# Three early blocks of gathers instead of two in a two-batch attention and deformable-convolution kernel, with more background calls while the early image is built

## The chip, the cores and the metric

The kernel runs on one core of one Trainium2 chip. The metric is the device time of one execution in microseconds (us). All data are float32.

## The reference, cut to what matters

The input x is two images of 256 channels, 64 x 64 pixels. Four layers follow one another:

- Layer 0: group norm, self-attention with 4 heads of 64 channels over the 4096 pixels, a projection, and the residual.
- Layer 1: a position term, added.
- Layer 2, the bottleneck: a 1x1 convolution to 64 channels, a 3x3 *deformable* convolution with a mask, a 1x1 convolution back to 256 channels, the residual and a ReLU.
- Layer 3: twice a group norm with ReLU and a 3x3 deformable convolution of 256 channels, whose offsets come from a 7x7 depthwise convolution and a 1x1 convolution; then the residual.

A deformable convolution reads its input at places that are known only at run time:

```python
off = off.reshape(B, KK, 2, H, W)
py = yy + ky + off[:, :, 0]; px = xx + kx + off[:, :, 1]
sampled = bilinear_gather(x, py, px)        # four corners, weighted
out = einsum('bckhw,ock->bohw', sampled, w)
```

## The kernel before, in words

`Net.run` calls `attention`, then `deform`. On TensorE (PE), VectorE (DVE), ScalarE (ACT) and GpSimd (POOL) the instructions stand in the order in which the Python code issues them. On SyncE (SP), which issues most of the plain DMAs, the order is left to a scheduler.

**Attention.** There are four units of work: (batch 0, heads 0 and 1), (batch 0, heads 2 and 3), and the same for batch 1. A unit has 256 steps n, 1024 in all, and the main loop takes two steps at a time, a *pair*. A step is a block of scores (L580, PE), its row minimum (L592, DVE), the exponentials (L598, ACT), their transposition (L610, PE) and copies (L627 DVE, L629 ACT), and the product with the values (L639, PE). POOL combines the parts of a block (L519 to L525).

What doesn't belong to a step is put between the steps in two ways. The dictionary `own` holds functions with the step at which they are due: loads, keys and values of the next unit, the projection, the first 1x1 convolution of layer 2. And `back` holds generators, the background, in order: `background(count)` (L661) goes through the list and takes up to `count` yields; a generator that yields False passes the turn to the next one. In a pair there are up to three such calls: one for each of the two steps without an own function (from unit 2 on), and one at the end of the pair.

In unit 2 `first_batch` joins the background: the deformable convolution of layer 2 for batch 0 (`conv`, with its gathers on POOL), and then `early_image` (L1180). That normalizes the result for batch 0 (L1192, ACT), stores it (L1197), transposes it (L1204, PE), copies it (L1209, DVE) into buffers `bfour`, and stores those as the image `img3` (L1214), from which layer 3 gathers: 25 yields, eight blocks i of one part for the activations and two for the transposes. In unit 3 `before` of batch 1 is put at the head of the list, and `early_samples` (L1218) at its end. That computes for the first `EARLY` blocks of layer 3 (a block is 512 pixels) the offsets (`offsets`, 28 matrix products per block at L805, then L825, L839 and the small DVE operations of `corners`), and queues 36 gathers per block: 9 taps by 4 groups of 128 pixels, each gather 128 rows of 4 KB. From then on `self.sample`, called once or twice at the end of a pair (11 times in 16 steps), issues one gather on POOL (L848) into one of the buffers in `free`, and on SP the store (L1261) of an earlier one to the scratch `samp_d` in HBM. There are three buffers (`xb`) until the offsets of the last early block are done, nine from then on. The main loop runs until n has passed 1028, the background is empty, nothing is due and no sample is left.

**Deform.** Layer 3, as 1152 samples s: two batches times two layers, each of 8 blocks of 36 samples. For a sample the kernel brings 128 x 1024 floats (`four`), weighs the four corners (ACT and DVE), transposes (L1508, PE), copies (L1517, ACT) and multiplies (L1527, PE). The 72 samples of the early blocks are loaded from `samp_d` (L1448, SP; the first 8 by POOL's queue); the others are gathered by POOL (L848, `four<-img,didx`). An early sample is weighed corner by corner: ACT scales the first (L1486), DVE adds the other three (L1496, three instructions). The other samples of the first layer of batch 0 are `paired`: ACT scales two corners at once (L1471), DVE adds the other two (L1477), and then one more of each (L1486, L1490). `gather` runs 8 samples ahead (`AHEAD`) into ten buffers.

Beside the first samples runs `conv` for batch 1: the second run of layer 2's deformable convolution, 144 steps, each with two gathers on POOL (`bfour<-img,bidx`, L848), a weighing (L1067) and two additions (L1077, L1078) on DVE, and after every fourth step a transposition (L1088) and its copy. It gathers seven steps ahead, into eight buffers. Its pace is set by a `Side`: at sample s it has had `rate * s + more(s)` yields; it has two yields per step, after 7 leading yields. When it is done, the second image is built from its result.

Of the kernel before, what the change touches and what calls it, by code (L numbers as in the profile page):

```python
# [25 lines left out]
K2 = 9  # L26
EPS = 1e-5
DWK = 7

EARLY = 2  # L30


GH, GW = H + 1, W + 2
# [31 lines left out]
class Net:  # L65
    def __init__(self, ctx, tc, a, out):
        self.tc, self.nc, self.a, self.out = tc, tc.nc, a, out
        nc = self.nc
        const = ctx.enter_context(tc.tile_pool(name="const", bufs=1))
        self.small = ctx.enter_context(tc.tile_pool(name="small", bufs=2))  # L70
        dram = ctx.enter_context(tc.tile_pool(name="dram", bufs=1, space=DRAM))

        self.ident = const.tile([P, P], F32, name="ident")
        make_identity(nc, self.ident)
        self.vec = const.tile([P, V_COLS], F32, name="vec")
        nc.sync.dma_start(self.vec, a["vec"])
        self.sel = const.tile([P, 32], F32, name="sel")
        self.shift = const.tile([P, DWK, 32], F32, name="shift")
        self.later = [(self.sel, a["sel"]), (self.shift, a["shift"])]

        self.img2, self.img3, self.x2d = [], [], []

        self.xn_d, self.xa_d = [], []
        for b in range(B):
            self.img2.append(dram.tile([GH * GW, 2 * CM], F32, name=f"img2_{b}"))
            self.img3.append(dram.tile([GH * GW, 2 * C], F32, name=f"img3_{b}"))
            self.x2d.append(dram.tile([C, HW], F32, name=f"x2d_{b}"))
            self.xn_d.append(dram.tile([C, HW], F32, name=f"xn_{b}"))
            self.xa_d.append(dram.tile([C, HW], F32, name=f"xa_{b}"))

        self.pos_d = dram.tile([C, HW], F32, name="pos_d")

        self.samp_d = [dram.tile([4 * K2 * P, 4 * C], F32, name=f"samp_d{i}") for i in range(EARLY)]
        self.sample = lambda: False
        self.early = {}
        self.share_d = [dram.tile([16, P], F32, name=f"share_d{n}") for n in range(2)]

        vec = self.vec
        self.bn_s = const.tile([P, 4], F32, name="bn_s")
        self.bn_t = const.tile([P, 4], F32, name="bn_t")  # L100
        rstd = self.rsqrt(vec[:, V_BNV : V_BNV + 4], 4)
        nc.vector.tensor_mul(self.bn_s, rstd, vec[:, V_BNG : V_BNG + 4])
        m = self.small.tile([P, 4], F32, name="bn_m")
        nc.vector.tensor_copy(m, vec[:, V_BNM : V_BNM + 4])

        nc.vector.tensor_sub(m[:, 1:2], m[:, 1:2], vec[:, V_DCNB : V_DCNB + 1])
        nc.vector.tensor_mul(m, m, self.bn_s)
        nc.vector.tensor_sub(self.bn_t, vec[:, V_BNB : V_BNB + 4], m)

        for v in (self.bn_s, self.bn_t):  # L110
            nc.vector.tensor_copy(v[CM:P, 0:2], v[0:CM, 0:2])
# [69 lines left out]
    def attention(self, bott):  # L181
# [5 lines left out]
        with ExitStack() as ctx:  # L187
# [489 lines left out]
            while n < last + 4 or back or more or any(own.values()):  # L677
                u, d = divmod(n, per_unit)
                if d == 0 and u < len(units):
                    plan_unit(u)  # L680
                    if u == 0:
                        back.append(prepare(1))
                    if u == 1:
                        back.append(bott.before(0, bt, ps))
                    if u == 2:
                        back.append(first_batch())
                    if u == 3:
                        back.insert(0, bott.before(1, bt, ps))
                        back.append(self.early_samples(bott, bt, held, xp, vp, kp, ps))

                def small(at):
                    steps = own.pop(at, ())
                    for f in steps:
                        f()
                    if not steps and u > 1:
                        background(1)

                if n - 1 in pts:
                    p = pts.pop(n - 1)
                    keep(n - 1, p, "ACT")  # L700
                    keep(n - 1, p, "DVE")
                ps.flush()
                sc = [scores(m) for m in (n + 2, n + 3) if m < last]
                for m in range(len(sc)):
                    lowest(n + 2 + m, sc[m])
                if n < last:
                    p = turn(e.pop(n))
                    keep(n, p, "DVE")
                if sc:
                    e[n + 2] = exponentials(n + 2, sc[0])  # L710
                if n < last:
                    keep(n, p, "ACT")

                small(n)
                if 4 <= n < last + 4:
                    attend(n - 4)
                    attend(n - 3)
                small(n + 1)
                if n < last:
                    pts[n + 1] = turn(e.pop(n + 1))  # L720
                if sc:
                    e[n + 3] = exponentials(n + 3, sc[1])
                if u or n % 8 == 0:
                    background(1)

                for _ in range(1 + (n % 16 in (10, 12, 14))):
                    more = self.sample()
                n += 2


    def corners(self, i, pt, mask, base, idx, w4, pool, w=None):

        nc = self.nc
        p = pool.tile([P, 4, K2, 2], F32, name="pos")
        off = pt[:, :, 0 : 2 * K2].rearrange("p j (k t) -> p j k t", t=2)
        nc.vector.tensor_tensor(p, off, base[:, 4 * i : 4 * i + 4], ALU.add)
        if mask:
            mk = pool.tile([P, 4, K2], F32, name="mask")  # L740
            nc.vector.tensor_scalar_max(mk, pt[:, :, 2 * K2 : 3 * K2], -87.0)
        yield False
        if mask:

            nc.scalar.activation(mk, mk, AF.Exp, scale=-1.0)

        nc.vector.tensor_scalar(p, p, float(H), -1.0, ALU.min, ALU.max)
        whole = pool.tile([P, 4, K2, 2], I32, name="whole")
        nc.vector.tensor_copy(whole, p)
        yield True  # L750
        f = pool.tile([P, 4, K2, 2], F32, name="floor")
        nc.vector.tensor_copy(f, whole)
        g = pool.tile([P, 4, K2, 2], F32, name="above")
        nc.vector.tensor_tensor(g, f, p, ALU.is_gt)
        yield False
        nc.vector.tensor_tensor(f, f, g, ALU.subtract)
        nc.vector.tensor_scalar_min(f, f, float(H - 1))
        if w is None:
            w = pool.tile([P, 2, 4, K2, 2], F32, name="wt")
        nc.vector.tensor_tensor(w[:, 1], p, f, ALU.subtract)  # L760
        yield False
        nc.vector.tensor_scalar(w[:, 0], w[:, 1], -1.0, 1.0, ALU.mult, ALU.add)
        at = g.rearrange("p j k t -> p (j k t)")[:, : 4 * K2]
        at = at.rearrange("p (j k) -> p j k", k=K2)
        nc.vector.scalar_tensor_tensor(
            at, f[:, :, :, 0], float(GW), f[:, :, :, 1], ALU.mult, ALU.add
        )
        nc.vector.tensor_scalar_add(idx, at, float(GW + 1))
        yield True
        if mask:  # L770
            nc.vector.tensor_scalar_add(mk, mk, 1.0)
            nc.vector.reciprocal(mk, mk)
            yield False
            for s in range(2):
                nc.vector.tensor_mul(w[:, s, :, :, 1], w[:, s, :, :, 1], mk)
            yield False
        for s in range(4):
            nc.vector.tensor_mul(w4[:, :, :, s], w[:, s % 2, :, :, 0], w[:, s // 2, :, :, 1])
        yield True
# [76 lines left out]
    class Bottleneck:  # L856
# [41 lines left out]
            self.od = wp.tile([P, 512], F32, name="bod")  # L898
            nc.gpsimd.memset(self.od, 0.0)

        def pools(self, ctx, gathers=5, sums=8):
            self.ahead = gathers - 1
            tc = self.net.tc
            return self.kept | {
# [275 lines left out]
    def early_image(self, bott, pools, ps):  # L1180

        nc, x2d = self.nc, self.x2d[0]
        sc, sh = self.norm_scale(bott.stats[0], bott.gmask, V_GN_G[0], V_GN_B[0], ps)
        yield True
        v = self.img3[0].rearrange("(y x) (s c) -> y x s c", x=GW, c=C)
# [31 lines left out]
    def early_samples(self, bott, pools, held, xp, vp, kp, ps):  # L1217
# [38 lines left out]
        def gather():  # L1256


            if len(stores) > 1 and len(free) < 3 or not gathers and stores:
                dst, four = stores.popleft()  # L1260
                nc.sync.dma_start(dst, four)  # L1261
                free.append(four)
# [8 lines left out]
        for i in range(EARLY):  # L1271
# [22 lines left out]
                load(i + 1)  # L1294
            if i + 1 == EARLY:
                free.extend(whole)
            for m in range(4 * K2):
                k, j = divmod(m, 4)
                gathers.append((self.samp_d[i][m * P : m * P + P, :], idx[:, j, k : k + 1]))

    def deform(self, bott):
# [5 lines left out]
        with ExitStack() as ctx:  # L1307
# [287 lines left out]


            last = Side(0, 1, bott.last(1, bott.kept, ps))
            seconds = Side(0, 0.9, second, lambda s: 2.5 * min(s, EARLY * BLOCK))
            stats[0] = self.norm_stats()
            images = []  # L1600
            for s in range(ALL + 12):
# [135 lines left out]
```

## Time and profile before

| what | us |
|---|---|
| median of 3 runs (5137.35 to 5144.84) | 5140.26 |
| the profiled execution | 5136.46 |
| its span, first to last instruction | 5134.7 |
| last exponential of attention (L598) starts | 2960.2 |
| first sample gather, last sample gather in attention | 2612.8, 2908.9 |
| first sample weighed in deform (L1486) | 2989.5 |
| first gather of the second `conv` on POOL | 2997.5 |

| engine | busy, us | share of the span |
|---|---|---|
| PE | 4802.3 | 94% |
| DVE | 4012.2 | 78% |
| ACT | 3255.6 | 63% |
| POOL | 2336.0 | 45% |

The profile is one execution. Its page gives the busy time of the engines, the span in 40 slices with the busy share of each in tenths, and groups of instructions: line, engine, operation, output and inputs, count, then busy time and mean ns of one, then the engine's idle time before them and what ended it. PEld is the weight load of PE; DMA is the mean share of the 16 DMA engines. "issue" is time in which an engine waited for nothing that the profile shows. Other views cut the same trace by window, by line, or list it in order of time; all their times count from the start of the span.

### The profile page before, as it was taken

The page shows a single profiled execution, that of the slowest core. Times are in us where ns is not written, and L with a number is a line of the kernel's source. Part 1 is how long each engine was busy: PE and PEld are TensorE (multiplying, and loading weights), DVE is VectorE, ACT ScalarE, POOL GpSimd, SP SyncE. Part 2 cuts the span into 40 slices and gives each one's busy share as a digit, 9 for nine tenths or more (in the row PEclk, how much of TensorE's full clock was granted, in tenths as well). Part 3 has the DMA queues.
Part 4 walks back from the last instruction along what each step waited for, and adds up shares of the span by engine and source line. Part 5 has one row for each costly group of instructions (what it writes and reads, how often), then busy time and mean ns, then how long its engine had stood idle before and what let it go on. Part 6 is the DMA issues. An engine that isn't in the chain of part 4 may idle for free. (4 is left out here: it accounts for less than half of the span.)

```text
span 5134.7 us, 100400 instructions
## 1 busy us (share of the span) xinstructions
PE 4802.3 (94%) x38200; PEld 2665.6 (52%) x38200; DVE 4012.2 (78%) x7281; ACT 3255.6 (63%) x5869; POOL 2336.0 (45%) x2256
## 2 busy tenths in 40 slices
PE   8999999999999999999999956679999999999998
PEld 5555565555565555565555523234444444454444
DVE  6878767878768888677766768867788888888888
ACT  5676656666667666666656622257876766666666
POOL 0111111111106777564023257775776666666665
PEclk9999999999999999999999978889999999999999
DMA  5231121111112333322557667679999999999998
GB/s 172 61 97 52 43 69 49 35 47 30 55 53 85 100 100 103 96 84 74 158 172 277 251 237 238 204 243 359 349 327 341 358 368 349 359 401 345 350 353 329
DMA packets 367026, 997.69 MB, mean 194 GB/s; under 512 B 61372, under 2 KB 98810, under 8 KB 366542
## 3 DMA queue, kind: packets, MB, share of 16 engines
q0 software_dynamic: 196560, 690.41, 37.7%
q1 hardware_dynamic: 169438, 300.73, 18.0%
q8 instruction: 300, 4.92, 0.4%
q14 instruction: 184, 1.51, 0.1%
q10 hardware_dynamic: 544, 0.13, 0.0%
HBM read 855.36 MB, written 127.35 MB: 191 GB/s over the span
## 5 line engine op out<-in xcount | busy, mean ns | idle before, releaser
L598 ACT ACTIVATE e<-sc,low 128x1024 f32<-128x1024 f32 x1024 | 1147.3, 1120 | 739.1 <-DVE low L592 736.2
L848 POOL DMA_INDIRECT four<-img,didx x1080 | 1163.2, 1077 | 558.1 <-issue 132.8
L592 DVE TENSOR_REDUCE low<-sc 128x1 f32<-128x1024 f32 x1024 | 1204.5, 1217 | 229.9 <-PE sc L580 225.3
L1527 PE MATMUL out<-st,wc 128*128 128x512 f32 x2304 | 1234.0, 618 | 118.2 <-ACT st L1517 100.7
L580 PE MATMUL sc<-k,qs 64*128 64x512 f32 x2048 | 998.0, 605 | 1.8 <-ACT e L598 1.4
L639 PE MATMUL av<-et,v 128*64 128x256 f32 x8192 | 996.6, 385 | 0.0
L580 PE MATMUL sc<-k,q 64*128 64x512 f32 x2048 | 977.0, 604 | 0.0
L519 POOL TENSOR_TENSOR o<-o,f 128x1024 f32<-128x1024 f32 x63 | 149.6, 2375 | 1763.4 <-DMA f<-share_d 966.5
L610 PEld LDWEIGHTS tt<-ident,e 64*128 64x128 f32 x16384 | 654.5, 139 | 512.4 <-issue 271.6
L629 ACT COPY et<-tt 128x512 f32<-128x512 f32 x1152 | 659.5, 585 | 171.4 <-PE tt L610 170.3
L1496 DVE SCALAR_TENSOR_TENSOR smp<-four,dw,smp 128x256 f32<-128x256 f32 x1296 | 627.2, 484 | 176.0 <-ACT smp L1486 144.9
L610 PE MATMUL tt<-ident,e 64*128 64x64 f32 x16384 | 726.5, 226 | 35.5 <-ACT et L629 18.3
L627 DVE COPY et<-tt 128x512 f32<-128x512 f32 x896 | 611.6, 683 | 161.7 <-PE tt L610 161.3
L639 PEld LDWEIGHTS av<-et,v 128*64 128x64 f32 x8192 | 553.2, 137 | 300.7 <-issue 47.8
L1508 PEld LDWEIGHTS pt<-ident,smp 128*128 128x128 f32 x2304 | 330.1, 144 | 661.6 <-issue 458.5
L848 POOL DMA_INDIRECT bfour<-img,bidx x576 | 583.5, 1013 | 183.5 <-issue 90.6
L1527 PEld LDWEIGHTS out<-st,wc 128*128 128x128 f32 x2304 | 389.9, 195 | 388.6 <-issue 201.2
L1471 ACT ACTIVATE four<-four,dwt 128x512 f32<-128x512 f32 x648 | 463.5, 715 | 192.6 <-DMA four<-img,didx 188.8
L1477 DVE SCALAR_TENSOR_TENSOR four<-four,dwt 128x512 f32<-128x512 f32 x648 | 483.8, 747 | 105.5 <-ACT four L1471 103.2
L1508 PE MATMUL pt<-ident,smp 128*128 128x128 f32 x2304 | 448.9, 277 | 27.2 <-DVE smp L1496 26.0
L580 PEld LDWEIGHTS sc<-k,qs 64*128 64x128 f32 x2048 | 346.2, 188 | 209.1 <-issue 116.3
L805 PE MATMUL pd<-x,wf 128*126 128x512 f32 x840 | 435.1, 600 | 0.0
(189 smaller groups left out, 4738.1 us busy)
## 6 DMA issues: line engine op xcount, KB each, us to landing
f<-share_d SPq DMA_DIRECT2D x128, 256.0 KB
four<-samp_d SPq DMA_DIRECT2D x64, 512.0 KB
xb<-xn SPq DMA_DIRECT2D x55, 512.0 KB
img<-imgt SPq DMA_DIRECT2D x96, 256.0 KB
four<-img,didx POOLq DMA_INDIRECT x1080
xa<-res SPq DMA_DIRECT2D x32, 512.0 KB
samp_d<-xb SPq DMA_DIRECT2D x32, 512.0 KB
xb<-in_x SPq DMA_DIRECT2D x20, 512.0 KB
```

Source lines behind the costliest of these rows:

```text
L580: nc.tensor.matmul(s[:, j, :], lhsT=q[u, i // 2][int(h != j)][halves[j], at : at + P], rhs=k[u][c][halves[j], h, :], start=True, stop=True,)
L592: nc.vector.tensor_reduce(low, s, AX.X, ALU.max, negate=True)
L598: nc.scalar.activation(e.rearrange("p j n -> p (j n)"), s, AF.Exp, bias=blk.low[:, g, c : c + 1], accum_out=blk.sum[:, g, c : c + 1],)
L610: nc.tensor.transpose(pt[:, m, :], e[half, m // 4, m % 4 * P : m % 4 * P + P], self.ident[half, half],)
L627: nc.vector.tensor_copy(dst, pt)
L629: nc.scalar.copy(dst, pt)
L639: nc.tensor.matmul(now["av"][halves[h], :], lhsT=v[u][c][:, m, halves[h]], rhs=ets[j][:, m, h, :], start=(m == 0), stop=(m == 7),)
L848: self.nc.gpsimd.indirect_dma_start(out=dst, out_offset=None, in_=img, in_offset=bass.IndirectOffsetOnAxis(ap=idx, axis=0),)
L1477: nc.vector.scalar_tensor_tensor(uv, four[:, 2 * C :], share(s, 1, 1), uv, ALU.mult, ALU.add)
L1496: nc.vector.scalar_tensor_tensor(smps[s], four[:, c], weight(s, c), smps[s], ALU.mult, ALU.add)
L1508: nc.tensor.transpose(pts[u][:, c, j * P : (j + 1) * P], smp[:, c * P : c * P + P], self.ident,)
L1527: nc.tensor.matmul(outs[ob], lhsT=wc[k][:, c, ob * P : ob * P + P], rhs=sts[u][:, c, :], start=(k == 0 and c == 0), stop=(k == K2 - 1 and ...
```

## The change

Five things change.

- `EARLY` is 3 instead of 2. A third block of offsets and 36 more gathers and stores are issued in attention; `deform` loads 108 early samples instead of 72, computes one block of offsets less, and weighs block 2 corner by corner instead of paired. The pool of corner buffers (`CORNERS`) grows from 11 to 12.
- `self.hurry` is 2 from the start of `early_image` until the offsets of the first early block are done, and 0 otherwise. The call at the end of a pair takes `1 + hurry` yields.
- `gather` of the early samples stores the oldest sample as soon as two are out, not only when fewer than three buffers are free.
- The second `conv` is paced over 108 samples: `1.6 * min(s, 108)` in place of `2.5 * min(s, 72)`, beside the unchanged rate of 0.9.
- `corners` keeps `whole` and `above` in one buffer, and attention's `conv` has 7 buffers `bsmp` instead of 8.

```diff
-EARLY = 2
+EARLY = 3
...
+        self.hurry = 0
...
-                    background(1)
+                    background(1 + self.hurry)
...
-        whole = pool.tile([P, 4, K2, 2], I32, name="whole")
+        whole = pool.tile([P, 4, K2, 2], F32, name="whole").bitcast(I32)
...
-        g = pool.tile([P, 4, K2, 2], F32, name="above")
+        g = whole.bitcast(F32)
...
-        def pools(self, ctx, gathers=5, sums=8):
+        def pools(self, ctx, gathers=5, sums=7):
...
     def early_image(self, bott, pools, ps):
         nc, x2d = self.nc, self.x2d[0]
+        self.hurry = 2
...
-            if len(stores) > 1 and len(free) < 3 or not gathers and stores:
+            if len(stores) > 1 or not gathers and stores:
...
                 free.extend(whole)
+            self.hurry = 0
             for m in range(4 * K2):
...
-            seconds = Side(0, 0.9, second, lambda s: 2.5 * min(s, EARLY * BLOCK))
+            seconds = Side(0, 0.9, second, lambda s: 1.6 * min(s, EARLY * BLOCK))
```

## The prediction, made before the changed kernel was built or run

> **What bounds the kernel now.** I read first the 40 slices of the page (128.4 us each).
>
> ```profile
> PE   8999999999999999999999956679999999999998
> DVE  6878767878768888677766768867788888888888
> POOL 0111111111106777564023257775776666666665
> DMA  5231121111112333322557667679999999999998
> ```
>
> PE is full in attention (slices 1 to 22) and DMA is full from slice 27 on. Between them, slices 23 to 26, neither is: that is where the first blocks of `deform` run beside the second `conv`, and it is the only stretch with room. The start times of `first` (L1486) give its blocks of 36 samples: block 0 begins at 2989.5, block 1 at 3152.6, block 2 at 3319.1, block 3 at 3437.1, block 4 at 3523.3; after that a block takes 57 to 61. So blocks 0 to 3 take 163, 167, 118 and 86 us, 534 together. The view of these windows:
>
> ```profile
> core 0: us, PE busy (x) PEld busy (x) DVE busy (x) ACT busy (x) POOL busy (x), PEclk, DMA share, GB/s
> 2989.00:3152.00 163.00, 89.68 (x271) 41.77 (x270) 132.03 (x315) 35.48 (x67) 117.34 (x114) 0.74 0.76 250
> 3152.00:3319.00 167.00, 116.36 (x361) 52.67 (x360) 146.93 (x334) 42.99 (x78) 129.06 (x125) 0.79 0.68 216
> 3319.00:3437.00 118.00, 77.33 (x240) 36.73 (x239) 77.94 (x166) 53.80 (x93) 91.47 (x87) 0.84 0.71 227
> 3437.00:3523.00 86.00, 69.17 (x237) 33.42 (x236) 61.51 (x141) 55.24 (x96) 51.80 (x48) 0.89 0.88 307
> ```
>
> POOL issues 125 gathers in 167 us and 87 in 118: 1.34 and 1.36 us each. A group of its own row shows why that is its limit although it is "busy" only 77%:
>
> ```profile
> L848 POOL DMA_INDIRECT bfour<-img,bidx x230 | 238.9, 1039 | 77.5 <-issue 37.2 <-DVE smp L1496 8.5 <-DMA x<-xn 8.3
> ```
>
> A gather takes 1.04 us and the timeline has 0.30 us behind each, whatever is named as releaser. So blocks 0 to 2 are bound by POOL's issue; DVE follows closely (147 of 167 us). Block 3 is mixed, with DMA at 0.88. What DVE does there (groups of 2989 to 3437):
>
> ```profile
> L1496 DVE SCALAR_TENSOR_TENSOR smp<-four,bw,smp 128x256 f32<-128x256 f32 x216 | 104.3, 483 | 9.9 <-DMA wc<-in_dcw 4.2 <-ACT smp L1486 0.5
> L1067 DVE TENSOR_TENSOR bfour<-bfour,bw 128x512 f32<-128x512 f32 x135 | 92.4, 685 | 34.6 <-DMA bfour<-img,bidx 34.5
> L1077 DVE TENSOR_TENSOR bfour<-bfour 128x256 f32<-128x256 f32 x135 | 57.0, 422 | 2.9
> L1078 DVE TENSOR_TENSOR bsmp<-bfour 128x128 f32<-128x128 f32 x135 | 39.5, 293 | 10.1
> ```
>
> The 0.2% that separates faster and slower from no change is 10 us here.
>
> **Deform: the gain.** `conv` has 144 steps of two gathers and two yields, after 7 leading yields. Its allowance at sample s is 0.9 s + 2.5 min(s, 72) before, 0.9 s + 1.6 min(s, 108) after. At s = 108 that is 277 yields before (135 steps, as the x135 above), 270 after (131 steps, with 7 more gathered ahead: 138 steps, 277 gathers). Before, POOL had also to issue 36 image gathers for block 2 and 8 for block 3; after, block 2 comes by SP from `samp_d`, so 8 remain. POOL: 285 x 1.34 = 382 us, and its first gather starts 8 us after block 0 (2997.5): 390. DVE: it was busy 132 + 147 + 78 = 357. Block 2 is no longer paired: 36 x (0.750 + 0.481) = 44 go, 36 x 3 x 0.483 = 52 come; four conv steps of 1.40 go (6). That is 359 us, and it can't be hidden by POOL any more: with the first wait for a gather (15.4 on the chain of waits), the 4.2 for `wc` and some 15 of small gaps it needs 393. Two engines at 390 and 393 that feed each other through 8 buffers: I take 400, 48 less than 448. Ends: 390 if they overlap perfectly, and 359/0.88 + 15 = 423 if DVE gets no fuller than in block 1, so -58 to -25. Block 3 has 12 conv steps instead of 9 and 47 gathers instead of 48; its DVE work rises by 5 us, which mostly lies beside the gathers: +3. Starting the second image some 8 samples later costs nothing: its 53 steps at 0.9 a sample end near s = 204, before 228 where they are forced. From block 4 on DMA is full and nothing changes. **Deform -45** (-58 to -20). The loads added on SP, 36 of 512 KB, replace gathers of the same size; DMA at 0.7 hides them. If that cover went, 36 x 1.58 us (57/36, the pace of full DMA) = 57 us would be at stake; that it is bound by POOL at 0.7 speaks against it.
>
> **Attention: what is paid.** PE is full there, so work added on PE is paid in full. Windows of attention (image; two blocks' offsets; sampling):
>
> ```profile
> 2449.00:2555.00 106.00, 100.25 (x1002) 60.46 (x1004) 72.88 (x118) 73.50 (x134) 9.22 (x7) 0.98 0.59 171
> 2578.00:2698.00 120.00, 116.93 (x1040) 65.67 (x1038) 70.45 (x133) 63.53 (x119) 28.52 (x27) 0.99 0.56 192
> 2698.00:2877.00 179.00, 174.62 (x1882) 105.08 (x1880) 126.55 (x205) 121.54 (x229) 58.67 (x56) 0.98 0.77 283
> ```
>
> (1) Block 2's offsets. By the exponentials of L598, 32 steps n of attention take 120 us with two blocks' offsets (second row), and 64 take 179 with sampling alone (third), 89.5 for 32. So a block costs (120 - 89.5)/2 = 15 us. PE's own row agrees:
>
> ```profile
> L805 PE MATMUL pm<-v,bx 128*126 128x512 f32 (+3 forms) x56 | 23.3, 573 | 0.0
> ```
>
> is 11.7 a block, and the seven shifted sums and the transposes add some 2.5. **+15** (13 to 17). The same work leaves `deform`, where PE was at 55 to 70%: no gain.
>
> (2) The squeezed image. Written out by the code's rules, the loop gives for before: image n = 852 to 886, first sample at 902, last at 1004; the trace has the first sample gather at 2612.8 and the last at 2908.9, between the exponentials of those n. With `hurry` a pair has up to five calls instead of three: image 852 to 866, blocks ready at 872, 882 and 888, samples 872 to 1026, and the loop ends at 1040 in both. The work is the same (64 transposes, 11.6 us of PE), but in 14 n it must pass SP, which the timeline shows full at such a pace:
>
> ```profile
> 2492.20 0.55 SPq L911 DMA_DIRECT2D bx<-x2d  x1
> 2492.79 0.50 SPq L1197 DMA_DIRECT2D xn<-bx  x1
> 2493.38 6.17 SPq L1214 DMA_DIRECT2D img<-bfour  x8
> 2499.65 0.55 SPq L911 DMA_DIRECT2D bx<-x2d  x1
> ```
>
> That is 7.45 us an image block, 60 for eight. Attention meanwhile takes 14 x 2.8 + 11.6 = 51. So the five `bfour` buffers fill and DVE's copies (L1209) wait some 9 us, with the steps n queued behind them on DVE; three calls in a row share one bank, where PE waited 0.58 + 0.37 us for the activation (timeline at 2491), 7 times 0.95 at worst, half of it beside the other wait. **+12.** Low end 0 (no gain: nothing is removed). High end: nothing overlaps, each block waits for 1.52 us of activation and two copies of 0.69, 8 x 2.9 = 23, plus SP's 9: 32, plus 6 us of landing (the upper end on the chain of waits) for each of two loads of `xs` that PE's matmuls follow directly: 44.
>
> The Trainium skill, "DMA: Bandwidth & Descriptors", section Specifications, puts the limit of HBM for one core at about 358 GB/s. An estimate by it: the image moves 16.8 MB (8 loads and 8 stores of 512 KB, 64 of 128 KB), which beside attention's own 50 GB/s (500 to 1000 us) would need 55 us, so about +4 where I have SP's +9, and the sum would be -19 by it. The trace has a slice at 401 GB/s, above that limit, so I let SP decide.
>
> (3) Sampling over 154 n instead of 102. The stretch 2698 to 2784 with samples takes 86 us for 32 n, the last, 2877 to 2961, with few, 84 for 31.5: 0. Storing as soon as two samples are out moves waiting from POOL (57 us before the gathers) to SP (160 us behind L1261 in 2700 to 2960); both have `f`, `q` and `xb` behind them, needed 11 n (30 us) or more later. 0, up to +5.
>
> (4) The end. The last sample is issued 22 n later, near attention's end, and its buffers become `deform`'s. Between 2961 and 2989 DMA is at 0.67; three or four samples of 1 MB at 283 GB/s are 13 us, mostly in the free third. **+4** (0 to 13). The bitcast, the seventh `bsmp` and the larger corner pool remove no instruction and lengthen no wait that I find: 0.
>
> **Sum.** -45 + 15 + 12 + 4 = -14. The profiled execution took 5136.5 (span 5134.7 and 1.8 around it), 3.8 under the median of 5140.3. I carry the difference to the median: 5126.
>
> **Rivals.**
> A, it is slower: the hurried image stalls attention. Place: PE waiting for L1192's activations, L1209's copies and the `xs` loads between n = 852 and 888. Price 44 in place of 12: -45 + 15 + 44 + 4 = +18, 5158. It decides from 26 us on, where the sum is zero. For it: DVE, ACT and PE are in order and SP is full already in the dense part. Against: PE was idle 13 us only from 2440 to 2700, with up to three steps a pair.
> B, DVE takes POOL's place: its work in blocks 0 to 2 isn't reduced at all (357 and 359). At 88% busy the gain is 22 and the sum +9: 5149. For it: 34.5 us of its idle time waits for landings. Against: those come from POOL being late.
> C, the squeeze is free and the two engines overlap well: -52 + 15 + 2 + 1 = -34: 5106. For it: SP's order isn't the program's, and `load(0)` was issued at 2478, 100 us ahead of its use.
> D, the early samples aren't done by attention's end and the loop goes on (the count says 1026 of 1040): a pair's 5.6 us each; 6 pairs would be +34 on the forecast, 5160.
>
> **Chances.** Forecast 0.42 (own range -28 to -2: 5112 to 5138), C 0.20, B 0.17, A 0.18, D 0.03. Faster by over 10 us: 0.72 of the forecast and all of C, 0.50. Within 10: the rest of the forecast and most of B, 0.27. Slower: A, D and the worse part of B, 0.23. The range leaves out the far ends of A and C: 5094 to 5162.
>
> **What would show it.** Right: first sample gather near exponential 874 and the last near 1026; attention's end 22 to 32 us later; 36 fewer `four<-img,didx` (1044), 100 loads from `samp_d` on SP; blocks 0 to 2 near 133 each, block 3 near 89; DVE above 88% there; 57 a block after. Wrong: blocks 0 to 2 over 141 (B), attention over 45 us later with PE idle at L1204 or L805 (A), bare gathers after the last exponential (D).

## The result, and the profile after

The changed kernel takes 5154.95 us (median of 10 runs, 5150.14 to 5164.9), the kernel before 5139.4 (10 runs): a ratio of 1.003, 95% interval 1.002 to 1.004. The forecast was 14 us faster; it is 15.5 us slower. The profiled execution took 5164.9, ten above its median.

The slices of the page, as in the prediction:

```profile
PE   8999999999999999999899966768999999999998
POOL 0111111111107777474023347775766666666666
DMA  5231121111113333322667787879989999999998
```

The full part of PE has a dent now, in slice 19 (2452 to 2581 us, counted from 0 as in the prediction): that is where the image and the offsets stand. The stretch between attention and full DMA is still there, slices 23 to 26. From the start times of the exponentials (step n of attention) and of `first` (the samples of deform), both lists by line:

| stretch | before | changed | difference |
|---|---|---|---|
| n = 848 to 912: image, offsets | 233.2 | 266.8 | +33.6 |
| n = 912 to the last exponential's start | 308.3 | 321.4 | +13.1 |
| from there to deform's first sample | 29.3 | 49.9 | +20.6 |
| deform, blocks 0 to 2 | 447.6 | 380.1 | -67.5 |
| deform, blocks 3 and 4 | 147.6 | 166.9 | +19.3 |

Up to block 4's end that is 18 us more (the two executions reach n = 848 at 2418.7 and 2417.7, so the seventh `bsmp` and the shared buffer of `corners` cost nothing up to there). The rest took 10 more in this execution. In the profiles of the experiments on chips of the same kind it takes 1552 to 1564 us with the changed deform and 1550 to 1554 with the old one, so part of that ten is scatter; a few us of it may be real, and no run looks into them.

The view by windows for blocks 0 to 4 of the changed kernel:

```profile
core 0: us, PE busy (x) PEld busy (x) DVE busy (x) ACT busy (x) POOL busy (x), PEclk, DMA share, GB/s
3055.90:3181.60 125.70, 81.85 (x235) 36.30 (x234) 109.07 (x270) 34.06 (x65) 90.41 (x85) 0.66 0.81 275
3181.60:3301.50 119.90, 84.27 (x262) 37.92 (x261) 113.33 (x249) 34.20 (x64) 92.79 (x90) 0.83 0.81 263
3301.50:3435.90 134.40, 96.81 (x321) 43.74 (x320) 126.50 (x292) 38.87 (x73) 103.76 (x98) 0.86 0.77 248
3435.90:3532.60 96.70, 72.47 (x237) 34.47 (x236) 68.27 (x146) 53.75 (x94) 63.27 (x62) 0.86 0.74 248
3532.60:3602.80 70.20, 62.47 (x236) 31.84 (x235) 52.93 (x118) 56.95 (x98) 38.83 (x37) 0.95 1.01 381
```

DVE is busy 349 of 380 us in blocks 0 to 2, 92%, and POOL issues a gather per 1.39 us: the two balance, as forecast. But POOL got through only 273 gathers there and left 62 to block 3 (it had 48 before); block 3 takes 10 us more. Block 4 takes 9 more: the second image starts 16 us into it (before: 6 us ahead of it), and one of its activations waits 5.9 us for its load. That these two make the +19 is read from the profile; no run separates them.

### The profile page after: what moved, and what is told of

Same layout as the page of the kernel before. It is cut to its first block, busy times and chain, and to the rows that moved or that the text cites. A ratio compares the mean times of both kernels' runs of the same rounds, so it can differ in the third digit from the quotient of the medians.

```text
span 5163.1 us, 100511 instructions
## 1 busy us (share of the span) xinstructions
PE 4819.4 (93%) x38200; PEld 2665.8 (52%) x38200; DVE 4020.7 (78%) x7317; ACT 3231.7 (63%) x5833; POOL 2334.1 (45%) x2256
## 5 line engine op out<-in xcount | busy, mean ns | idle before, releaser
L849 POOL DMA_INDIRECT four<-img,didx x1044 | 1122.2, 1075 | 560.3 <-issue 136.3
L849 POOL DMA_INDIRECT bfour<-img,bidx x576 | 589.5, 1023 | 185.1 <-issue 92.3
L1474 ACT ACTIVATE four<-four,dwt 128x512 f32<-128x512 f32 x612 | 437.7, 715 | 152.0 <-DMA four<-img,didx 149.5
L1480 DVE SCALAR_TENSOR_TENSOR four<-four,dwt 128x512 f32<-128x512 f32 x612 | 456.9, 746 | 84.1 <-ACT four L1474 82.1
L806 PE MATMUL pd<-x,wf 128*126 128x512 f32 (+3 forms) x812 | 417.8, 597 | 0.0
```

What stands on the lines that cost most here:

```text
L806: nc.tensor.matmul(pd[:m, r0 * W : r1 * W], lhsT=wt(s, t), rhs=src[:, (y + r0 - y0) * W : (y + r1 - y0) * W], start=(n == 0), stop=(n == l ...
L849: self.nc.gpsimd.indirect_dma_start(out=dst, out_offset=None, in_=img, in_offset=bass.IndirectOffsetOnAxis(ap=idx, axis=0),)
```

## The experiments

Theory T after the first look: deform gains what was forecast, and attention loses it in four places: the third block of offsets on PE, the squeezed image, late f tiles while samples run (`f` holds the factors with which POOL combines a block's parts; SP loads it from `share_d`), and the end. Each ratio is to the kernel before, timed on the same chip. The groups came from five chips; on three of them the kernel before takes 5141 to 5143 us, on two 5316 and 5320, so kernels are compared within a group.

### First group (before: 5142.74)

**e1_lazy**, the old store rule.

```diff
-            if len(stores) > 1 or not gathers and stores:
+            if len(stores) > 1 and len(free) < 3 or not gathers and stores:
```

> The changed kernel with the store rule of before (a sample is stored only when fewer than three buffers are free); all else as changed. Theory T, from the trace of the changed kernel against the one before: the loss has four places: third block of offsets on PE in attention (+15), the squeezed image (+18), late f tiles while sampling (+12), and the last f tile, which SP issues behind sample stores (+21); deform gains 48 as forecast. Under T the store rule moves only part of the last two: 0 to 10 us less than the changed kernel, the wait of the last combine (22.7 us in the changed kernel) still 10 to 23. Rival R1, the store rule alone makes both the sampling and the end late: 25 us less or more, and the first sample of deform 30 us after the last exponential instead of 49.

5156.37 us, 1.0029 (1.0018 to 1.0039): as the changed kernel. n = 912 to the last exponential 318.8 instead of 321.4, the end 48.2 instead of 49.9. The store rule is not the cause, save for 2 to 3 us; R1 falls.

**e2_hurry2**, before with hurry alone.

```diff
-                    background(1)
+                    background(1 + self.hurry)
...
+        self.hurry = 2
...
+            self.hurry = 0
```

> The kernel before with hurry alone (two early blocks, old stores, old pace). T: steps n = 848 to 912 take 250 us instead of 233 (stalls of PE behind activations, copies and image stores), all samples out by n = 974, nothing else changes: 5152 to 5160 where before is 5139, deform as before. Rival R2, the calls in a row are free and the loss of the changed kernel there is the third block of offsets: 5134 to 5144.

5162.42 us, 1.0043 (1.0029 to 1.0057): **hurry alone costs 20 us.** n = 848 to 912 takes 254.4 instead of 233.2; deform's blocks 0 to 2 take 450.0 instead of 447.6, so deform is unchanged. So R2 falls, and in the changed kernel 12.4 of that stretch are the third block. Windows of before, then of this kernel, then of the changed one:

```profile
2418.00:2470.00 52.00, 45.90 (x439) 27.13 (x438) 36.51 (x74) 32.91 (x59) 4.41 (x3) 0.97 0.33 92
2470.00:2520.00 50.00, 47.17 (x491) 28.65 (x489) 35.47 (x54) 35.51 (x63) 4.36 (x3) 1.00 0.70 208
```

```profile
2418.00:2470.00 52.00, 43.82 (x389) 25.42 (x387) 33.42 (x64) 30.32 (x54) 4.91 (x4) 0.90 0.45 131
2470.00:2520.00 50.00, 37.00 (x333) 21.83 (x329) 27.21 (x50) 25.22 (x45) 2.56 (x2) 0.86 0.75 221
```

```profile
2418.00:2470.00 52.00, 43.94 (x392) 25.75 (x388) 33.69 (x74) 30.91 (x55) 4.91 (x4) 0.90 0.44 126
2470.00:2520.00 50.00, 36.56 (x312) 21.48 (x312) 25.93 (x41) 26.21 (x45) 4.34 (x3) 0.86 0.81 240
```

In the second window PE is busy 37 of 50 us instead of 47, and the granted clock is 0.86 instead of 1.00. What each of the two is worth shows over the whole of n = 848 to 912, where both kernels run the same instructions on PE (before, then this kernel):

```profile
2418.70:2651.90 233.20, 220.13 (x2052) 127.26 (x2054) 152.35 (x269) 138.81 (x251) 27.43 (x23) 0.99 0.48 146
2420.80:2675.20 254.40, 226.20 (x2052) 129.34 (x2054) 152.10 (x273) 138.84 (x251) 47.28 (x44) 0.94 0.63 206
```

PE's idle time rises from 13 to 28 us, and the same 2052 instructions keep it busy for 6 us more at the lower clock. So of the 21 us some 15 are waiting and some 6 the clock. What PE waits for, in the view of waits of this kernel from 2449 to 2520 (us in total, times, longest):

```profile
PE pm L1206 <- ACT bx L1194: 12.2, 8, 5.7
DVE bfour L1211 <- DMA img<-bfour: 7.3, 2, 6.6
ACT bx L1194 <- DMA bx<-x2d: 5.6, 1, 5.6
```

PE's transposes wait for the activation, that for its load, and DVE's copy for a store of the image.

**e3_nohurry**: `self.hurry = 2` becomes 0 in the changed kernel.

> The changed kernel with hurry 0 throughout. By the count the samples then run from n = 902 to 1056 and the loop ends at 1060 instead of 1040. T: the stretch of the image is as before plus 15 for the third block, the last exponential 18 us earlier than in the changed kernel (near 2988), but some 30 samples are left then, at 3.3 us of DMA each: first sample of deform near 3080 instead of 3056, total 15 to 30 us over the changed kernel. Rival R4, hurry is what costs and samples after attention's end are cheap: 15 us or more under the changed kernel.

5183.49 us, 1.0081 (1.0068 to 1.0095), the slowest of the group and 27 us over the changed kernel, where T had 15 to 30. n = 848 to 928 is 294.0 instead of 279.2 before: the third block costs 14.8 without crowding. Deform's first sample comes 81.9 us after the last exponential. R4 falls: samples after attention's end are dear.

**e4_actlast**: the last block's shares and f loads on ACT's queue.

```diff
-                    nc.sync.dma_start(d, t)
+                    end = self.u + 1 == len(units) and self.i == 15
+                    queue = nc.scalar if end else nc.sync
+                    queue.dma_start(d, t)
...
-                        nc.sync.dma_start(
+                        queue.dma_start(
```

> The changed kernel, but the last block's shares and its two f loads are issued from ACT's queue, not SP's, so that they don't stand behind the sample stores. T: the last combine waits under 8 us instead of 22.7, the first sample of deform comes 33 to 38 us after the last exponential instead of 49, total 11 to 16 us under the changed kernel. Rival R3, it is not SP's order but the sample data that fill the DMA engines: f lands about as late, total within 5 us of the changed kernel.

5155.12 us, 1.0026 (1.0017 to 1.0035): nothing gained, as R3 had the total. The edit did only a part of what it was meant to do: the last combine waits 15.3 us for its f instead of 22.7, where T had under 8. The end falls from 49.9 to 42.7, and block 0 rises from 125.8 to 131.4. T's reading of the end was wrong for the changed kernel: the late f isn't on its chain of waits. These are the longest pieces of that chain from 2990 to 3110 (start, us, what):

```profile
3000.22 13.93 DMA bx<-img,bidx
3014.17 7.61 DMA samp_d<-bx
3022.26 5.00 DMA samp_d<-xb
3029.15 9.69 DMA four<-samp_d
3039.12 9.66 DMA four<-samp_d
3049.78 6.03 DMA x<-xn
3066.93 5.79 DMA bfour<-img,bidx
```

The last samples land after attention's end, their stores follow, and only then are the buffers free that deform's first loads need. (The samples go through eight buffers by then, not nine: three `xb`, two `v`, two `bx` and one `k`.) POOL's last sample gather starts at 3010.4, 4.5 us after the start of the last exponential (before: 51 us ahead of it), and the first gather of the second conv 58 us after it (before: 37). In the kernel before, the chain runs at this place through attention's last products on PE (below), and the loads follow them:

```profile
2966.58 4.04 PE av L639 x32
```

From the last exponential to POOL's first load of a sample it is 11.5 us there and 21.9 in the changed kernel; from that load to the first sample 17.8 and 27.9.

### Second group (before: 5316.35)

**e5_pace**, before with the pace alone: `1.6 * min(s, 3 * BLOCK)`.

> The kernel before with the pace of the changed kernel alone (second conv over 108 samples, two early blocks). Theory T2: in blocks 0 to 2 the sum of POOL's gathers decides (about 321 at 1.34 us by either pace), so the pace only moves time between blocks: blocks 0 and 1 near 125 each, block 2 near 170, block 4's end within 10 us of before, total 5130 to 5150. Rival R5, it is the gentler pace and not the third block that brings deform's gain: block 4 ends 20 us or more earlier.

5308.59 us, 0.9981 (0.9964 to 0.9998). Blocks 0 to 2 take 158.6, 144.6 and 198.0. The pace moves time between blocks, as T2 had it (f4_before_act, with the old pace, has 204.1, 212.6 and 110.9 on a chip of the same kind), though the sizes are not T2's. What it brings, 0.2%, is at the edge of the measurement, so R5's gain isn't there on this chip; on the kind of chip of the first group the pace alone was not run.

**e6_spread**, the changed kernel with the calls spread over attention's own conv.

```diff
-                    background(1 + self.hurry)
+                    background(1 + (512 <= n < 812 and n % 8 == 0))
```

> The changed kernel with hurry replaced: no extra calls in the image, but one extra call in every fourth pair from n = 512 to 812, while attention's own conv runs. By the count the image then stands at n = 814 to 836 and the samples at 846 to 1002. T2: the 21 us that hurry alone cost come from crowding the image into a few pairs, so they go; the samples end before attention does, so the end costs 29 us again instead of 50 and the last f isn't late; third block of offsets still +13. Total 25 to 35 us under the changed kernel, 5120 to 5130. Rival R6, any earlier image costs the same because SP and the transposes are paid wherever they stand: within 10 us of the changed kernel.

5333.57 us, 1.0028 (1.001 to 1.0045). T2's 25 to 35 us are against the changed kernel, beside which it was timed in the third group.

**e7_spread_act**, the same with sample stores on ACT's queue (`nc.scalar.dma_start(dst, four)`) and the old store rule.

> As e6_spread, with the sample stores on ACT's queue instead of SP's and the store rule of before. T2: shares to f loads takes 2 to 5 us instead of 9 to 14 while sampling, the stretch from n = 928 to the last exponential is 3 to 10 us shorter; total 0 to 10 us under e6_spread. Rival R7, issuing on ACT delays the exponentials: 5 us or more over e6_spread.

5290.23 us, 0.9941 (0.9919 to 0.9963): the first kernel clearly under the one before, and 43 us under e6_spread, where T2 had at most 10. n = 928 to the last exponential takes 267.4 instead of e6_spread's 292.8. R7 falls.

**e8_spread_p19**, `1.9` in place of `1.6` in e6_spread.

> As e6_spread, with 1.9 in place of 1.6, so that the second conv ends with sample 108. T2: DVE binds blocks 0 to 2, which take 15 to 20 us more; blocks 3 and 4 (167 us in the changed kernel, 148 before) fall to 125 to 140, since they lose conv's gathers and weighing: 5 to 20 us under e6_spread. Rival R8, the work is only moved: within 5 us of e6_spread.

5353.05 us, 1.0061 (1.004 to 1.0082). Blocks 0 to 2 take 501 instead of 446, blocks 3 and 4 133 instead of 162. The second half of T2's statement was right, the first wrong by 35 us: at this pace blocks 0 to 2 lose 55 us and blocks 3 and 4 win 29 back. R8 falls with it.

### Third group (before: 5320.14)

**f1_changed**, the changed kernel again.

> The changed kernel once more, as the control for the three beside it: the runs so far came from two chips, on the second of which the kernel before takes 5316 us instead of 5143, so only kernels timed side by side are compared. 0.2 to 0.4% over before on any chip.

5326.58 us, 1.0013 (0.9999 to 1.0027): a little under what was expected.

**f2_spread**, e6_spread again.

> The changed kernel with the extra calls spread over attention's own conv (n = 512 to 812) instead of crowded into the image. Theory T3: crowding costs some 20 us and the late end some 10, so 10 to 30 us under the control. Rival R6, earlier calls cost the same wherever they stand: within 8 us of the control.

5330.84 us, 1.0025 (1.0012 to 1.0038): no better than the control, as R6 had it, and T3 falls on this chip. In the profile, n = 848 is reached 55 us later and the rest of attention takes 60 less: earlier calls cost about what they save.

**f3_spread_act**, e7_spread_act again.

> The spread calls, and the sample stores on ACT's queue with the store rule of before. T3: 0.3 to 0.8% under before on any chip, as it was 0.59% under on the second one; the stretch from n = 928 to the last exponential at most as long as without samples' waits (86 us per 32 steps).

5285.27 us, 0.9935 (0.9914 to 0.9956), as expected. n = 928 to the last exponential takes 268.2, about 90 per 32 steps, where T3 had 86.

**f4_before_act**, before with ACT's queue for the sample stores.

> The kernel before with its sample stores on ACT's queue alone. T3: what sampling costs attention by way of SP is small there (102 steps, f tiles 9 to 13 us late), so 0 to 10 us under before, and the rest of what the spread kernel with ACT stores gains comes from the third block. Rival R9, the store queue is the whole of that gain: as far under before as the spread kernel with ACT stores.

5298.5 us, 0.9955 (0.9941 to 0.9969). On this chip some 60% of f3_spread_act's gain is the store queue alone. T3 expected at most 10 us of it, and it is 22; R9's whole isn't reached either.

### Fourth group (before: 5141.8)

**g1_hurry_act**, the changed kernel with ACT's queue and the old store rule.

> The changed kernel with hurry as it is, but the sample stores on ACT's queue with the store rule of before. T3: the stretch from n = 912 to the last exponential loses its long waits of PE (it was 322 us against 309 before on the first chip), the last combine no longer waits; the squeezed image keeps its cost. 12 to 35 us under the changed kernel, at or under before. If spreading is worth nothing, it equals the spread kernel with ACT stores (the last of these four) within 8 us.

5159.58 us, 1.0035 (1.0023 to 1.0047). n = 912 to the last exponential falls to 309.4, before's 308.3: of the +13, the store rule is 2.6 (e1_lazy has 318.8) and SP's queue the other 9 to 10. Yet the total doesn't fall, where T3 had it at or under before, since the samples still end 13.5 us after the last exponential starts: the end is 37.6, and block 0 takes 143.4 instead of 125.8.

**g2_image_pool** and its control **g3_hurry2** (e2_hurry2 again): `(nc.sync, nc.gpsimd)[s].dma_start(...)` for the image stores.

> The kernel before with hurry alone, and half of the image stores (s = 1) issued by POOL, which is idle there, instead of SP. T4: hurry's 21 us come from SP: loads and stores of the image queue up, ACT and DVE wait for them, PE idles and its granted clock falls to 0.86. With half the issues gone n = 848 to 912 takes 236 to 246 us instead of 254, 8 to 18 us under the control. Rival R10, it is the three calls in a row that share one bank and wait for each other: within 5 us of the control.

> Control for the kernel beside it: before with hurry alone. 0.3 to 0.5% over before.

5166.27 and 5164.94 us, both 1.0047 (1.0033 to 1.0061); n = 848 to 912 254.7 and 253.0. T4 falls: SP's issue, which the prediction priced, isn't what hurry waits for. R10's total comes out here, and the fifth group tests its cause.

**g4_spread_act**, e7_spread_act on this chip.

> The spread calls with ACT stores once more, beside the others: 0.3 to 0.8% under before on any chip; on a chip like the first one (before near 5143) the lesser end, since SP's waits cost less there.

5136.35 us, 0.9992 (0.9983 to 1.0001): 23 under g1_hurry_act beside it, and level with before, where 0.3 to 0.8% under it was expected. Its samples end 35 us ahead of the last exponential, and the end plus block 0 is 162.7 instead of 181.0. Its image takes some 22 steps n, against 15 with hurry and 33 before, and stands earlier. The window of its image, then that of e2_hurry2's:

```profile
2361.00:2440.00 79.00, 72.82 (x729) 43.89 (x725) 51.96 (x73) 54.28 (x96) 9.21 (x7) 0.98 0.78 227
2445.00:2528.00 83.00, 62.25 (x521) 36.30 (x518) 45.43 (x91) 43.46 (x74) 4.34 (x3) 0.81 0.71 207
```

At this pace PE is idle 6 of 79 us, with hurry 21 of 83.

### Fifth group (before: 5141.19)

**h1_split**, e2_hurry2 with its two extra calls apart from each other.

```diff
                     attend(n - 4)
+                    background(self.hurry // 2)
                     attend(n - 3)
...
                     pts[n + 1] = turn(e.pop(n + 1))
+                    background(self.hurry // 2)
...
-                    background(1 + self.hurry)
+                    background(1)
```

> The kernel before with hurry alone, but its two extra calls are spread within the pair (one between the two products with the values, one after the second transposition) instead of standing in a row behind the last one. T5: PE's idle time in n = 848 to 912 (28 us with the calls in a row, 13 before) comes from calls in a row that share one bank and one activation, and falls to 13 to 20; the stretch takes 236 to 246 us, the total is 0 to 0.3% over before. Rival R11, any five calls in a pair cost this, since image loads, activations and copies can't follow faster: idle 24 us or more, total 0.35 to 0.5% over before.

5162.31 us, 1.0035 (1.0021 to 1.0049); n = 848 to 912 255.0. R11 holds and T5 falls: it isn't calls in a row, it is five calls a pair. The waits from 2449 to 2520 have moved to the loads:

```profile
ACT bx L1196 <- DMA bx<-x2d: 15.7, 3, 7.4
```

**h2_split_act**, g1_hurry_act with the calls apart.

> The changed kernel with the calls spread within the pair and the sample stores on ACT's queue with the store rule of before. T5: 10 us or more under the changed kernel, within 0.1% of before. R11: 0.25 to 0.4% over before.

5153.89 us, 1.0024 (1.0015 to 1.0034): as the changed kernel, and at the lower end of R11's 0.25 to 0.4%, not within T5's 0.1%.

## Why the prediction was wrong

Three steps failed: sampling, put at 0; the end, put at 4; and the squeezed image, put at 12 by a limit of SP that wasn't the limit. Together they cost 55 us instead of 16.

**Deform: right in sum, partly by luck.** Forecast -45, measured -67.5 + 19.3 = -48. POOL's bound went, DVE became as full as POOL, 36 gathers fewer (1044) and 100 loads by SP, all as said. Two terms inside were off and happen to cancel. Blocks 0 to 2 took 380 and not 400: DVE was busy 349 us and not 359, the 7 us allowed for imperfect overlap weren't needed, and a dozen of the 285 gathers slid into block 3. Blocks 3 and 4 took 19 more and not 3: block 3 had 62 gathers for the 47 reckoned, and the second image's later start, put at nothing, stands where block 4 took 9 more. The group of DVE's weighing shows how its wait for landings shrank (34.6 us before, for 135):

```profile
L1068 DVE TENSOR_TENSOR bfour<-bfour,bw 128x512 f32<-128x512 f32 x129 | 88.1, 683 | 9.0 <-DMA bfour<-img,bidx 8.8 <-issue 0.2
```

**The third block's offsets: right.** Forecast +15; 12.4 and 14.8 by two comparisons.

**The squeezed image: the place right, the size and the cause not.** Forecast +12, measured +21. The step took SP's 7.45 us an image block as the limit; half of SP's stores on POOL changed nothing. Spreading the calls in the pair changed nothing either. What the runs leave is the image's own chain at that pace (load, activation, transposes, copy, store, with two input buffers and five output buffers), in which PE waits some 15 us more, and that PE is granted less clock there, some 6 us, for which the sum had no term. The Trainium skill, "TensorE: Matmul & The Clock Gate", Part 1, says that an idle window of about 3.4 us halves PE's clock until it has been busy for about as long. The traces agree in kind: 0.86 in these 50 us, where PE waits up to 5.7 us at a time (e2_hurry2), against 1.00 in the kernel before. Which link of the chain comes first stays open: no run had more buffers for the image.

**Sampling: priced at 0, measured +13.** The step moved the waits from POOL to SP and held that the queue behind them had 30 us to spare. It hasn't: the f tiles wait there, the combine on POOL waits for them, and DVE's copies of the next block's products (L471, into `o`) wait for the combine. The step counted 11 n from f's load to its use; that is the way to the projection (steps 16 and 27 of a block in the code). But the combine reads the only buffer `o`, and the next block's first product overwrites that at step 22: 6 n, some 17 us. Waits of n = 928 to the end, before and changed:

```profile
DVE o L471 <- POOL avs L525: 10.6, 4, 5.1
```

```profile
DVE o L472 <- POOL avs L526: 24.8, 6, 6.1
```

With the old store rule (e1_lazy) this wait is 21.7 us, with the stores off SP as well (g1_hurry_act) 13.2, and the 13 are gone. On the second kind of chip the store queue is worth more, with 72 samples too (22 us in f4_before_act), but not by this path. e6_spread and e7_spread_act ran on one such chip and differ in the queue and the store rule alone; from n = 928 to the last exponential they take 292.8 and 267.4 us. In e6_spread's waits there (2780 to 3072) there is none of DVE for the combine. These are the largest with a releaser that the trace doesn't name ("remote"); in e7_spread_act 1.8 us of ACT's and 0.9 of DVE's are left:

```profile
ACT et L630 <- remote: 32.5, 5, 7.6
DVE o L472 <- remote: 13.0, 2, 6.5
```

Why the queue of the stores matters to them stays open.

**The end: priced at 4, measured 21.** The step counted bytes against the free third of DMA. What matters is the chain: last gather, store, buffer, deform's first loads, each of 5 to 14 us. Half of the 21 is that the first load is issued later, half that the loads take longer. Rival D had the right kind of fear and the wrong test: the count said that the loop ends at 1040 in both, but the last exponential is issued with n = 1020, so a last sample at n = 1026 is behind it already in the code. g4_spread_act, whose samples end 35 us ahead of the last exponential, has an end of 30.0 us.

With these three sizes in place of 12, 0 and 4 the forecast's sum becomes -45 + 15 + 21 + 13 + 21 = +25, where the profile has +18 up to block 4's end and the medians 15.5. Rival A's total, +18, was close, but it was one mechanism at 44; the runs show three of 13 to 21, so that hit is luck. The limit of HBM that the prediction weighed did not come to bear: by it the image would have cost less than by SP, and it cost more than either.

## What to carry to other kernels

Work squeezed into a stage that PE fills can cost more than its PE time: here the image's work stayed the same and cost 21 us more, 15 in waits and 6 in clock, and the queue that the samples' stores use had someone behind it. Stores that must wait for a gather belong on a queue where nobody urgent stands behind them. And what is done "early" must have landed, been stored and freed its buffers before the next stage starts: count to the last landing, not to the last issue.

## What the runs showed of the hardware

Chips differ by more than the change: the kernel before took 5142.74, 5141.8 and 5141.19 us on three and 5316.35 and 5320.14 on two. In all eight profiles from the latter, engines wait for something that the trace doesn't name ("remote"), 45 to 65 times and 205 to 344 us in sum; in the twelve from the others never. In deform POOL then waits for buffers that DVE holds; f4_before_act, 3100 to 3380:

```profile
POOL bfour L848 <- DVE bsmp L1078: 60.3, 22, 11.6
ACT bst L1090 <- remote: 49.6, 4, 18.0
```

On such a chip the store queue is worth 0.45% by itself (f4_before_act); on one of the first kind the changed kernel's total gained nothing by it (g1_hurry_act). What makes the two kinds differ stays open.

A gather of 128 rows holds POOL for about the same time at both sizes used here: 1023 ns for rows of 1 KB, 1075 ns for rows of 4 KB by the page's groups of the changed kernel, and 0.30 us stand behind each where POOL isn't held up. So in the second conv POOL is full at some 77% "busy".
